# A two-layer post-LN network on one core: the same instructions, ordered by a planner with other costs and other shifts

## The chip, the core and the metric

The kernel runs on one core of one Trainium2 chip. The metric is device microseconds of one execution, here the median of 14 executions. Five engines of the core work side by side, each strictly in the order of its own queue: TensorE (PE in the profile; PEld is its loading of weights), VectorE (DVE), ScalarE (ACT), GpSimd (POOL) and SyncE (SP), which here only issues DMAs. Semaphores tie the queues together.

## The reference, cut to what matters

x has 8 batches of 512 tokens of 128 features, in float32. Four blocks follow each other, each with a residual sum and a LayerNorm behind it.

```python
x = L0_attn_x
x = _layernorm(x + _L0_attn_ref(x, ...))   # linear attention, then its own FFN
x = _layernorm(x + _L0_ffn_ref(x, ...))    # first mixture of experts
x = _layernorm(x + _L1_attn_ref(x, ...))   # softmax attention with rotary positions
x = _layernorm(x + _L1_ffn_ref(x, ...))    # last mixture of experts

# _L0_attn_ref: 16 heads of 64, 64 random features
qf = ratio * (exp(q_dash - diag - max_over_features) + EPS_KERN)
kf = ratio * (exp(k_dash - diag - max_over_all) + EPS_KERN)
kv = einsum('bnhm,bnhd->bhmd', kf, v)
num = einsum('bnhm,bhmd->bnhd', qf, kv)
den = einsum('bnhm,bhm->bnh', qf, sum(kf, axis=1))
out1 = _layernorm(x + attn_out)
h = elu(out1 @ W1 + b1)                    # 512 wide
return _layernorm(out1 + h @ W2 + b2)

# _L0_ffn_ref: 8 experts of width 64, the best 2 of each token
gates = _top_k_softmax(cos_scores + route_scores, 2)
h = gelu(einsum('bsd,edh->bseh', x, w1) + b1)
out = einsum('bse,bsed->bsd', gates, einsum('bseh,ehd->bsed', h, w2) + b2)

# _L1_attn_ref: 16 heads of 8
q, k = q * cos + rotate_half(q) * sin, k * cos + rotate_half(k) * sin
attn = softmax(einsum('bhqd,bhkd->bhqk', q, k) / sqrt(8))
out = einsum('bhqk,bhkd->bhqd', attn, v)   # then @ wo.T + bo

# _L1_ffn_ref: 8 experts of width 176, the best 2 of each token, and a shared expert
h = silu((x @ w1 + b1) * (x @ w3 + b3))    # per expert
y = sum over the 2 chosen experts of weight * (h @ w2 + b2)
return y + silu((x @ sw1 + sb1) * (x @ sw3 + sb3)) @ sw2 + sb2
```

## The kernel before, in words

**Stages.** 512 tokens of a batch are four blocks (NT) of 128 tokens by 128 features.

- *Keys.* `keys` runs once for all eight batches at the start: keys, their features and their sums, in scratch memory that is later used again (matmuls at L677, L687 and L716, VectorE at L684 and L693).
- *First layer, per batch* (`linear_attention_and_ffn`, stage 0): for each of the four blocks query features (PE L921, L931; ACT square and exponential; VectorE reductions L928 and L937; POOL product L945; VectorE L951), transposes (L961) and eight matmuls with the folded keys (L969); then a LayerNorm (`moments` and `layernorm`: VectorE L874 and L883, POOL power L876), an FFN (PE L994, L1005) and two more LayerNorms.
- *First mixture, per batch* (`first_mixture`, stage 1): transposes (L629, in the helper `transpose4`, which every stage uses), a router (L1040 and a row of short VectorE steps), one Gelu over all hidden units, gates spread over rows by DMA, matmuls L1075, L1089, L1091.
- *Attention, per batch* (`softmax_attention`, stage 2): projections (PE L1115; the rotary steps on VectorE and POOL L1121, L1122; VectorE and POOL L1127 split each value into a high part and a rest), four DMAs that write the parts to DRAM (`put`, L1104), eight that read them back as a layout of 32 rows per head (`get`, L1107), and the value projection (L1137). Then sixteen steps of four score matmuls on 32 rows each (L1183), two exponentials on ACT (L1189) and eight value matmuls (L1195); after each four steps transposes and a normalisation (L1202 to L1208); at the end the output projection (L1155) with its residual sum (L1161).
- *Last mixture.* Batches 0 to 3 and 4 and 5 are two groups in which tokens are sorted by expert (`sort`, stage 3: router L1309, counting matmuls L1563, eight indirect DMAs of POOL that scatter 128 token rows each to DRAM, L1506, and the shared expert, L1594 and L1603). When a group is sorted, `tiles` (stage 4) runs over tiles of 256 sorted rows: SP fetches the tile's expert weights (L1528) and rows, PE transposes (L1657) and multiplies (L1663, L1671), `gated` is between (VectorE L1548, L1552), and SP stores the rows. `combine` (stage 5) gathers each token's two rows with eight indirect DMAs of POOL (L1514) and adds them (L1690). Batches 6 and 7 go through `dense_mixture` (stage 3) instead: all experts for all tokens (PE L1364, L1389, VectorE L1375).

**The planner.** No instruction is issued where it is written. `Schedule` records each call, or each group of calls inside `nc.together()`, as a `Work` with its engine, a planned duration `us`, for DMAs a time `lands` until the data have landed, and the works before it, found from overlapping operands. `nc.do` records a DMA with a duration and landing time written by hand. A work also has a `part`: the stage and the batch or group. Stage 6 is the layout of the last mixture's weights, stage 7 the folded keys of a batch, and None is the rest.

`issue` takes the works in the order that `order` returns. This has three steps. `latest_alone` walks back from the due time of each work (40 us per batch) and gives its latest start, were it alone. To this `order` adds a shift per part from the table `URGENT`. `forward` then plans: each engine has a list of ready works, sorted by this urgency; again and again the earliest possible start is taken, among equals the most urgent, and the PSUM banks (8 banks, handed to works as they start) are assigned on the way.

```python
best = self.forward([u + shift[w.part] for u, w in zip(urgency, self.works)])
...
start, found, own = max(free[e], at[i]), (), ()
...
free[e] = start + us
done = start + max(us, w.lands)
```

`ROUNDS` is 0, so there is no search when the kernel is built: table and costs fix the order. The costs are in `Schedule.us` by engine and operation, `HANDOVER` (from one engine to another), `KEPT` (within one) and `REFILL` (PE changing between a full tiling and a 32-wide one). A planned start is not a time on the chip: it only sets the order in each queue, and the chip waits by semaphores wherever the plan was wrong.

Line numbers in this document up to the result are those of this kernel.

Of the kernel before, what the change touches and what calls it, by code (L numbers as in the profile page):

```python
# [84 lines left out]
URGENT = {  # L85
    (0, 0): 4.8, (0, 1): 6.8, (0, 2): -10.9, (0, 3): 9.3, (0, 4): 10.3, (0, 5): 17.3, (0, 6): 1172, (0, 7): 48.3,
    (1, 0): -1314.2, (1, 1): -963.6, (1, 2): 66.8, (1, 3): -32.6, (1, 4): -720.6, (1, 5): 37.5, (1, 6): 70.3,
    (1, 7): 692.6, (2, 0): -832.2, (2, 1): -87.5, (2, 2): -790.6, (2, 3): -167.1, (2, 4): -29.3, (2, 5): 50.4,
    (2, 6): -1456.9, (2, 7): -6.2, (3, 0): 52.7, (3, 1): 77.9, (3, 2): 703.5, (3, 3): 72.2, (3, 4): -20.5,
    (3, 5): 856.5, (3, 6): 600.2, (3, 7): 580.1, (4, 0): -19, (4, 1): 11.1, (5, 0): 131.5, (5, 1): 134.1,  # L90
    (5, 2): -1202, (5, 3): 1752.2, (5, 4): 2071, (5, 5): 1790.6, (6, 0): -359.3, (7, 0): -253.4, (7, 1): -263,
    (7, 2): 384.7, (7, 3): 186.4, (7, 4): -1273.5, (7, 5): -8.4, (7, 6): 784, (7, 7): 744.1, None: 19.1,
}
# [8 lines left out]
class Work:  # L102


    def __init__(self, engine):
        self.engine, self.calls, self.us, self.lands = engine, [], 0.0, 0.0
        self.before, self.after = set(), []
        self.tiles, self.part = set(), None
        self.outs, self.apart = 1, None


class Schedule:
# [4 lines left out]
    KEPT = {"PE": 0.0, "DVE": 0.12, "ACT": 0.13, "POOL": 0.12, "SP": 0.0}  # L117
    REFILL = 0.1
    NAMES = {"tensor": "PE", "vector": "DVE", "scalar": "ACT", "gpsimd": "POOL", "sync": "SP"}

# [67 lines left out]
    @staticmethod  # L188
    def us(engine, method, args, kwargs, work):

        aps = [a for a in (*args, *kwargs.values()) if isinstance(a, bass.AP)]
        n = max(math.prod(a.shape[1:]) for a in aps)
        if method == "dma_start":
            us = max(0.1, math.prod(aps[0].shape) * 4 / 300e3)
            work.lands = 2.3 + us
            return us if engine == "SP" else 0.4
        if engine == "PE":
            n = math.prod(args[0].shape[1:])
            if method == "transpose":
                return 0.11  # L200
            return 2 * max(0.1115, n / 1200 + 2.5e-3)
        if engine == "DVE":
            pointed = any(isinstance(a, bass.AP) and a.shape[-1] == 1 for a in args[2:])
            return 0.07 + n * 1.03e-3 + (0.06 if pointed else 0.0)
        if engine == "ACT":
            if any(a is AF.Gelu or a == AF.Gelu for a in args[2:]):
                return 4.5
            each = (kwargs.get(k) for k in ("bias", "scale"))
            return 0.07 + n * 0.83e-3 + 0.1 * sum(isinstance(a, bass.AP) for a in each)
        if method == "tensor_tensor" and args[3] == ALU.pow:  # L210
            return 1.0
        if method == "memset":
            return 0.1 + n * 0.75e-3
        return 0.1 + n * 2.26e-3
# [121 lines left out]
    def forward(self, urgency):  # L336
# [7 lines left out]
        clear = [0.0] * BANKS  # L344
        tiling, span, starts = None, 0.0, []
        free = dict.fromkeys(self.HANDOVER, 0.0)
        open_, at, ready = [len(w.before) for w in works], [0.0] * len(works), {e: [] for e in free}
# [3 lines left out]
        for _ in works:  # L351
            best = None
            for e, waiting in ready.items():
                kept, found_here = set(), None
                for entry in waiting:
# [4 lines left out]
                    for n in works[i].tiles:  # L360
# [13 lines left out]
                        if place is None:  # L374
                            start = NEVER
# [18 lines left out]
            if e == "PE":  # L394
                if self.tilings[i][0] != tiling or start > free[e]:
                    us += self.REFILL
                tiling = self.tilings[i][1]
            free[e] = start + us
            done = start + max(us, w.lands)
# [56 lines left out]
def kernel(ctx: ExitStack, tc: tile.TileContext, i: dict, out: bass.AP):  # L456
# [652 lines left out]
    def projections(xb, b=None):  # L1109
# [3 lines left out]
        for n, name in ((0, "q"), (1, "k")):  # L1113
# [10 lines left out]
            if b is not None:  # L1124
# [3 lines left out]
                for a, half in enumerate((high, r)):  # L1128
                    rows_d = halves_d[b, n].rearrange("p (u v) n -> p u v n", v=2)
                    nc.do(  # L1130
                        "sync", put, (rows_d[:, :, a] if n == 0 else rows_d[:, a],), (half,),
                        1.7, 4.0, ("halves", b, n),
                    )
# [30 lines left out]
    def softmax_attention(b, dst):  # L1164
# [3 lines left out]
        for j in range(4):  # L1168
            for n, to in ((1, kx), (0, qx)):
                nc.do(  # L1170
                    "sync", get, (to[:, j, :].bitcast(F32),),
                    (halves_d[b, n].rearrange("(r j) c n -> r j c n", j=4)[:, j],), 0.85, 3.2,
                )
# [3 lines left out]
        def probabilities(j, kt):  # L1177

            halves = [nc.banks(2, 4 * (kt % 2) + 2 * a) for a in range(2)]
            with nc.together(0.3):  # L1180
                for g in range(4):
# [429 lines left out]
    def tiles(n, end, group, rows_d, weights_of):  # L1611
# [37 lines left out]
        for j in range(most):  # L1649
            which, first = (listed[0:1, k, j : j + 1] for k in range(2))  # L1650
            w, x = weights_of.next(), tile2("m_x").rearrange("p (t d) -> p t d", d=D)
            nc.do("sync", fetch_weights, (w,), (w_d, which), 0.9, 4.5)
            nc.do("sync", fetch_tokens(group), (x,), (rows_d, first), 0.9, 3.3, ("tiles", group))
            xt = psb("xt")[:, 0:TR]
# [23 lines left out]
            )  # L1678
            nc.do("sync", store_tokens(group), (rows_d,), (y, first), 0.9, 3.3, ("tiles", group))

# [167 lines left out]
```

## Time and profile before

| what | value |
|---|---|
| median of 14 runs | 1201.43 us (1194.74 to 1209.97) |
| the profiled execution | 1207.79 us; span from first to last instruction 1205.9 us |
| mean granted TensorE clock | 0.942 of full speed |
| HBM read, written | 80.81 MB, 55.41 MB; 113 GB/s over the span |
| exponentials of the scores (ACT L1189) | 256 of 1030 ns: 245.5 us |
| value matmuls (PE L1195) | 1024 of 664 ns, overlapping: 157.7 us |
| score matmuls (PE L1183) | 512 of 537 ns, overlapping: 77.9 us |
| product with the key sums (POOL L945) | 32 of 2428 ns: 77.7 us |
| scatters and gathers (POOL L1506, L1514) | 48 of 1012 ns and 48 of 1043 ns |
| chain that ended last | PE 19% of the span, DVE 9%, issue 3%, ACT 2%, others 1% or less |

The profile is of one execution; its own time lies 6.4 us above the median. A busy share is the time in which at least one instruction of an engine was under way. PE's matmuls overlap in the pipeline, so the mean of one is longer than what a row of them costs each. The chain of work that ended last leaps over long stretches here, because nearly every step of it was released by an instruction that was itself ready early; so the reading goes by stretches and by what each PE instruction waited for.

The stretches in order: up to about 210 us the keys; from there to about 930 us the first layer of one batch, the attention of another and, late, sorted tiles overlap; the sorted tiles run from 767 to 1120 us; from 930 to 1010 us the last sort and the start of attention of batch 6; to 1150 us attention of batches 6 and 7 beside tiles and the dense mixture of batch 6 (L1364 from 1057 us); and then the last dense mixture.

### The profile page before, as it was taken

The page shows a single profiled execution, that of the slowest core. Times are in us where ns is not written, and L with a number is a line of the kernel's source. Part 1 is how long each engine was busy: PE and PEld are TensorE (multiplying, and loading weights), DVE is VectorE, ACT ScalarE, POOL GpSimd, SP SyncE. Part 2 cuts the span into 40 slices and gives each one's busy share as a digit, 9 for nine tenths or more (in the row PEclk, how much of TensorE's full clock was granted, in tenths as well). Part 3 has the DMA queues.
Part 4 walks back from the last instruction along what each step waited for, and adds up shares of the span by engine and source line. Part 5 has one row for each costly group of instructions (what it writes and reads, how often), then busy time and mean ns, then how long its engine had stood idle before and what let it go on. Part 6 is the DMA issues. An engine that isn't in the chain of part 4 may idle for free. (4 is left out here: it accounts for less than half of the span.)

```text
span 1205.9 us, 16926 instructions
## 1 busy us (share of the span) xinstructions
PE 1077.6 (89%) x5764; PEld 610.1 (51%) x5764; DVE 869.6 (72%) x1935; ACT 717.5 (60%) x959; POOL 443.5 (37%) x381
## 2 busy tenths in 40 slices
PE   8999999898889998999997997999898757899994
PEld 4444444674654554554454454466652523555553
DVE  5866666879997599497689579469765682674795
ACT  2354355465448758767765664876467646667652
POOL 0234222243444262253373533214344671210362
PEclk9999999999889999998998898899988967999998
DMA  7029901123051041033133105455713351574241
GB/s 219 27 52 307 323 12 71 62 84 81 27 184 44 19 169 51 27 130 101 34 123 114 44 35 180 147 146 163 237 36 104 96 195 51 155 235 132 68 117 57
DMA packets 104605, 134.40 MB, mean 111 GB/s; under 512 B 19474, under 2 KB 62285, under 8 KB 104513
## 3 DMA queue, kind: packets, MB, share of 16 engines
q1 hardware_dynamic: 101137, 126.41, 33.3%
q0 software_dynamic: 3072, 6.30, 1.8%
q8 instruction: 47, 0.77, 0.3%
q10 hardware_dynamic: 304, 0.56, 0.2%
q14 instruction: 45, 0.37, 0.1%
HBM read 80.81 MB, written 55.41 MB: 113 GB/s over the span
## 5 line engine op out<-in xcount | busy, mean ns | idle before, releaser
L1189 ACT ACTIVATE scratch<-ps 128x1024 f32<-128x1024 f32 x256 | 245.5, 1030 | 64.9 <-PE ps L1183 45.5
L1195 PE MATMUL ps<-scratch,vv 128*32 128x512 f32 x1024 | 157.7, 664 | 6.5 <-ACT scratch L1189 3.9
L945 POOL TENSOR_TENSOR scratch<-scratch 128x1024 f32<-128x1024 f32 x32 | 77.7, 2428 | 154.3 <-ACT scratch L942 126.7
L1183 PE MATMUL ps<-qx,kx 32*128 32x512 f32 x512 | 77.9, 537 | 29.6 <-ACT scratch L1189 15.0
L682 ACT ACTIVATE scratch<-ps 128x1024 f32<-128x1024 f32 x32 | 32.7, 1023 | 91.8 <-PE ps L677 91.8
L1183 PEld LDWEIGHTS ps<-qx,kx 32*128 32x128 f32 x512 | 29.8, 196 | 112.5 <-ACT scratch L1189 51.1
L969 PEld LDWEIGHTS ps<-scratch 128*128 128x128 f32 x512 | 62.9, 198 | 19.3 <-issue 12.7
L969 PE MATMUL ps<-scratch 128*128 128x128 f32 x512 | 66.7, 285 | 6.0 <-DVE f_ln_ve L874 3.9
L921 PE MATMUL ps<-wq,scratch 128*128 128x512 f32 x128 | 65.9, 627 | 2.8 <-ACT scratch L926 1.1
L931 PE MATMUL ps<-wqf,scratch 128*128 128x512 f32 x128 | 65.2, 620 | 0.3 <-DVE scratch L941 0.3
L1663 PE MATMUL ps<-scratch 128*128 128x256 f32 x228 | 60.6, 406 | 3.7 <-DVE scratch L1548 3.0
L693 DVE SCALAR_TENSOR_TENSOR scratch<-k_ssq,ps 128x1024 f32<-128x1024 f32 x32 | 38.8, 1213 | 33.3 <-PE ps L687 26.0
L1506 POOL DMA_INDIRECT x_d<-scratch,slots x48 | 48.6, 1012 | 37.0 <-DVE f_nb L939 12.8
L677 PE MATMUL ps<-scratch 128*128 128x512 f32 x128 | 60.2, 613 | 1.2 <-ACT scratch L669 0.7
L876 POOL TENSOR_TENSOR f_ln_rs<-f_ln_ve,nhalf 128x4 f32<-128x4 f32 x24 | 28.2, 1175 | 86.4 <-DVE f_ln_ve L874 72.7
L1514 POOL DMA_INDIRECT scratch<-x_d,slots x48 | 50.1, 1043 | 25.2 <-issue 13.3
L716 PE MATMUL ps<-scratch,x_sb 128*128 128x512 f32 x128 | 59.2, 595 | 0.0
L687 PE MATMUL ps<-scratch 128*128 128x512 f32 x128 | 58.6, 600 | 0.0
L937 DVE TENSOR_REDUCE f_mxq<-ps 128x16 f32<-128x1024 f32 x32 | 38.9, 1215 | 21.3 <-PE ps L931 10.0
L725 POOL TENSOR_TENSOR scratch<-scratch 128x1024 f32<-128x1024 f32 x7 | 16.5, 2364 | 100.2 <-PE ps L687 76.2
L684 DVE TENSOR_REDUCE k_ssq<-scratch 128x16 f32<-128x1024 f32 x32 | 38.9, 1215 | 19.8 <-ACT scratch L682 19.8
L1663 PEld LDWEIGHTS ps<-scratch 128*128 128x128 f32 x228 | 43.3, 203 | 15.6 <-DVE scratch L1548 4.2
(290 smaller groups left out, 2529.8 us busy)
## 6 DMA issues: line engine op xcount, KB each, us to landing
halves_d<-scratch SPq DMA_DIRECT2D x32, 512.0 KB
scratch<-w_d SPq DMA_DIRECT2D x38, 386.0 KB
x_d<-scratch SPq DMA_DIRECT2D x28, 512.0 KB
scratch<-g_d SPq DMA_DIRECT2D x68, 128.0 KB
qx<-halves_d SPq DMA_DIRECT2D x32, 256.0 KB
kx<-halves_d SPq DMA_DIRECT2D x32, 256.0 KB
scratch<-x_d SPq DMA_DIRECT2D x38, 128.0 KB
x_d<-scratch SPq DMA_DIRECT2D x38, 128.0 KB
```

What stands on the lines that cost most here:

```text
L677: nc.tensor.matmul(kp_ps[:, a, :], xT[:, t * P : (t + 1) * P], wk[:, a * 512 : (a + 1) * 512], start=True, stop=True,)
L687: nc.tensor.matmul(dp_ps[:, a, :], xT[:, t * P : (t + 1) * P], wkf[:, a * 512 : (a + 1) * 512], start=True, stop=True,)
L716: nc.tensor.matmul(xp_ps[:, a, :], x_of(b)[:, t, :], ek[:, t, a * 512 : (a + 1) * 512], start=(t == 0), stop=(t == NT - 1),)
L921: nc.tensor.matmul(qp[:, a, :], xT[:, t * P : (t + 1) * P], wq[:, a * 512 : (a + 1) * 512], start=True, stop=True,)
L931: nc.tensor.matmul(dp[:, a, :], xT[:, t * P : (t + 1) * P], wqf[:, a * 512 : (a + 1) * 512], start=True, stop=True,)
L945: nc.gpsimd.tensor_tensor(pr, eq, zr[:, 0:HM], ALU.mult)
L969: nc.tensor.matmul(at_ps[:, 0:D], qnT[:, c, :], kvo[:, c, :], start=(c == 0), stop=(c == 7))
L1183: nc.tensor.matmul(halves[g // 2][:, g % 2, :], kx[quarter, j, kt * P : (kt + 1) * P], qx[quarter, j, :], start=True, stop=True, tile_posi ...
L1189: nc.scalar.activation(pr[:, 2 * a : 2 * a + 2], sc, AF.Exp, scale=1.0 / math.sqrt(HD2))
L1195: nc.tensor.matmul(av[32 * g : 32 * g + 32, :], vv[:, kt, head_columns(4 * g + j)], pr[:, g, :], start=(kt == 0), stop=(kt == NT - 1), til ...
L1514: inst = tc.nc.gpsimd.indirect_dma_start(out=to, out_offset=None, in_=rows_d, in_offset=bass.IndirectOffsetOnAxis(ap=slots_, axis=0))
L1663: nc.tensor.matmul(to, w[:, c : c + P], xf, start=True, stop=True)
```

## The change

All calls, operands and dependences stay. What changes is what the planner is told:

- the table `URGENT`: 64 other shifts;
- a new term: VectorE's planned work becomes longer by 0.7 of the time in which it overlaps the last planned POOL `tensor_tensor` (`SHARED`, `shares`, `shared`);
- the planned cost of every DMA by `dma_start`: 0.45 us of its queue, landing after 2.4 us and 1 us for each 100,000 elements, in place of at least 0.1 us and 2.3 us and 1 us for each 300 KB;
- VectorE's reciprocals 0.06 us longer;
- the costs by hand of `put` (1.7 and 4.0 us to 0.6 and 4.2), `get` (0.85 and 3.2 to 0.6 and 4.4), the fetch of weights (0.9 and 4.5 to 0.4 and 4.2), the fetch and the store of rows (0.9 to 0.4), and the four score matmuls (0.3 to 0.335).

```diff
 URGENT = {
-    (0, 0): 4.8, (0, 1): 6.8, (0, 2): -10.9, (0, 3): 9.3, (0, 4): 10.3, (0, 5): 17.3, (0, 6): 1172, (0, 7): 48.3,
-    (1, 0): -1314.2, (1, 1): -963.6, (1, 2): 66.8, (1, 3): -32.6, (1, 4): -720.6, (1, 5): 37.5, (1, 6): 70.3,
...
-    (7, 2): 384.7, (7, 3): 186.4, (7, 4): -1273.5, (7, 5): -8.4, (7, 6): 784, (7, 7): 744.1, None: 19.1,
+    (0, 0): -50.3, (0, 1): -68.4, (0, 2): -44.4, (0, 3): 45.9, (0, 4): 9.7, (0, 5): 244.3, (0, 6): 1789,
+    (0, 7): 819.9, (1, 0): -1119.5, (1, 1): -1339.6, (1, 2): 82.9, (1, 3): -73.4, (1, 4): -541.6, (1, 5): 348.9,
...
+    (7, 1): 436.8, (7, 2): 707.9, (7, 3): 442.5, (7, 4): -1380.9, (7, 5): -634.9, (7, 6): 1112.9, (7, 7): 550.9,
+    None: -76.1,
 }
@@ class Schedule
     REFILL = 0.1
+    SHARED = 0.7
@@ us
         if method == "dma_start":
-            us = max(0.1, math.prod(aps[0].shape) * 4 / 300e3)
-            work.lands = 2.3 + us
-            return us if engine == "SP" else 0.4
+            work.lands = 2.4 + math.prod(aps[0].shape) / 100e3
+            return 0.45
...
-            return 0.07 + n * 1.03e-3 + (0.06 if pointed else 0.0)
+            return 0.07 + n * 1.03e-3 + (0.06 if pointed or method == "reciprocal" else 0.0)
...
+        work.shares = method == "tensor_tensor"
@@ forward
+        shared = (0.0, 0.0)
...
+            elif e == "DVE":
+                us += self.SHARED * max(0.0, min(start + us, shared[1]) - max(start, shared[0]))
+            elif w.shares:
+                shared = (start, start + us)
@@ projections, softmax_attention
                     nc.do(
                         "sync", put, (rows_d[:, :, a] if n == 0 else rows_d[:, a],), (half,),
-                        1.7, 4.0, ("halves", b, n),
+                        0.6, 4.2, ("halves", b, n),
...
-                    (halves_d[b, n].rearrange("(r j) c n -> r j c n", j=4)[:, j],), 0.85, 3.2,
+                    (halves_d[b, n].rearrange("(r j) c n -> r j c n", j=4)[:, j],), 0.6, 4.4,
...
-            with nc.together(0.3):
+            with nc.together(0.335):
@@ tiles
-            nc.do("sync", fetch_weights, (w,), (w_d, which), 0.9, 4.5)
-            nc.do("sync", fetch_tokens(group), (x,), (rows_d, first), 0.9, 3.3, ("tiles", group))
+            nc.do("sync", fetch_weights, (w,), (w_d, which), 0.4, 4.2)
+            nc.do("sync", fetch_tokens(group), (x,), (rows_d, first), 0.4, 3.3, ("tiles", group))
...
-            nc.do("sync", store_tokens(group), (rows_d,), (y, first), 0.9, 3.3, ("tiles", group))
+            nc.do("sync", store_tokens(group), (rows_d,), (y, first), 0.4, 3.3, ("tiles", group))
```

## The prediction

> **What bounds the kernel now.** I read four views in turn: the page's busy shares, the busy time by stretch, the timeline of single stretches, and the sources of single lines.
>
> ```profile
> span 1205.9 us, 16926 instructions
> PE 1077.6 (89%) x5764; PEld 610.1 (51%) x5764; DVE 869.6 (72%) x1935; ACT 717.5 (60%) x959; POOL 443.5 (37%) x381
> ...
> PEclk9999999999889999998998898899988967999998
> ```
>
> TensorE (PE) is busy 89% of the span, but a busy PE is not a PE at its peak, so I count its work. Back to back at full clock the chain of waits shows eight 128x128 matmuls in 0.89 us, six of 128x256 in 1.30 and four of 128x512 in 1.72. All groups priced like this (0.90 for eight of L1195, 0.30 for four of L1183) are an estimated 936 us. Starts of neighbouring groups lie 48 us further apart in small steps under 0.25 us (changes between full and 32-wide tilings above all), 98 us are true waits at full clock, and stretches at half clock cost 109 us more; about 15 us are the two ends. The clock records have 20 stretches at 0.50, 141 us together, which is the mean of 0.942 again: (1 - 0.942) / 0.5 x 1206 = 140. In them PE did 66.6 us of full-clock work, so 66.6 of the 109 us is the clock and 42 is waiting. Waits are thus 98 + 42 = 140 us, and the clock adds 66.6 / 140 = 0.47 us for each.
>
> ```profile
> 0.00:210.00 210.00, 202.11 (x615) 91.83 (x616) 137.88 (x186) 91.78 (x94) 55.26 (x34) 1.00 0.47 145
> ...
> 750.00:930.00 180.00, 161.34 (x1016) 102.42 (x1018) 118.04 (x309) 123.07 (x179) 63.29 (x69) 0.93 0.46 139
> 930.00:1010.00 80.00, 53.37 (x274) 28.14 (x272) 52.47 (x167) 42.25 (x65) 49.20 (x51) 0.74 0.40 129
> 1010.00:1150.00 140.00, 133.56 (x841) 79.87 (x838) 90.74 (x221) 98.98 (x148) 26.50 (x22) 0.99 0.45 134
> 1150.00:1206.00 56.00, 37.92 (x179) 23.50 (x178) 39.34 (x93) 22.60 (x43) 24.99 (x21) 0.92 0.28 86
> ```
>
> Columns: stretch, its length, busy us (and instructions) of PE, weight loads, VectorE (DVE), ACT and POOL, clock, DMA. The keys stage (first row) is full: no order can save much there. The worst stretch is 930 to 1010: PE busy 53 of 80 us, clock 0.74. No engine is full there; it is a passage of short dependent steps, in which attention of batch 6 waits for its projections and the last sort for its router.
>
> ```profile
> 872.84 1.07 PE L1195 MATMUL ps<-scratch,vv 128*32 128x512 f32 x8
> ...
> 876.61 2.93 PE L1663 MATMUL ps<-scratch 128*128 128x256 f32 x6 [2.70 <-DVE scratch L1548]
> ...
> 879.33 1.06 PE L961 MATMUL ps<-ident,scratch 128*128 128x128 f32 x4
> ```
>
> What an order can lose is seen here: PE waits 2.7 us for an L1663 while the L961 behind it had its inputs. Engines take their queues strictly in order, so a late head holds back all behind it.
>
> **The change part by part.** The instructions are the same: 4869 pieces of work with the same dependences, 17 activation tables loaded before and after. Only the order on the five engines and the PSUM banks differ, because the planner's costs and 64 shifts differ. I laid every instruction of the trace on its piece of work, and then both orders beside each other.
>
> *1. Late heads that go.* For each gap over 0.3 us before a PE group I looked whether one of the eight groups behind had all inputs. Such gaps hold 94.7 us that a ready group could have taken. For 39.4 us of it the new order has that ready group first (the L961 above is one). Term: -39.4 us of waits.
>
> *2. Waits that come.* For each PE group that needs another engine's result of an earlier PE group, I took the steps between at their durations in the trace, without queues, less the PE work that lies between the two. What is left is a wait that the order cannot avoid: 85.4 us before, 86.9 us after. 21.5 us go and 23.0 come. They come where the mixture of batch 7 starts behind L1005 of its first layer (L1005 to L629 and L1040: +8.9), at the last routers (L1309 to L1563: +4.3), at L931 to L961 (+2.3) and L994 to L1005 (+2.6); they go at L1115 to L1183 (-5.1), the sorted tiles (-3.3) and L1594 to L1603 (-4.2). The 23.0 is a floor. Measured waits are 140 against 85.4, a factor of 1.64, so the other end is 38. I take the middle, 30: nothing puts the truth nearer to one end.
>
> *3. Clock.* Net waits -39.4 + 30.5 = -9, and 0.47 of it by the clock: -4. Both ends: (-39.4 + 23) x 1.47 = -24 and (-39.4 + 38) x 1.47 = -2.
>
> *4. Changes of tiling.* They go from 363 to 377. A change cost about 0.10 us (L1195 to L1183 0.095 in the mean, L1183 to L1195 0.136): +1.4; the ends, +1.3 to +1.9, don't matter.
>
> *5. Batch 6.* Its projections (L1115) stand at 758.9 us of PE work instead of 763.8, ahead of L1005 and the router of batch 5. VectorE must have done 815 us of its work before the first scores now and 819 before, so the start gains little beyond term 2. I take 0; ends -7 (L1115 earlier by 4.9, x 1.47) and the first rival.
>
> *6. Queues of SP and POOL.* SP's 491 issues are moved with their steps; L1104 takes 548 ns and L1107 594 ns in the median, and the queue is far from full. The scatters of batches 0 and 1 come about 45 to 60 us of PE work earlier, behind which POOL has slack. Cost 0: what they feed (the tiles) starts at the same place, 628 against 621 us of PE work. Ends -3 and +3, the mean length of three such issues of about 1.0 us.
>
> *7. The port term.* The plan now lengthens VectorE's work under a POOL tensor_tensor. It moves nothing by itself; its effect is in terms 1 and 2. Its accuracy can be read here.
>
> ```profile
> L883 DVE SCALAR_TENSOR_TENSOR f_ln_nm<-f_ln_mv,f_ln_rs x16: 147/155/2268, 247.5 to 970.9; 128x4 f32<-128x4 f32 x16
> ...
> L928 DVE TENSOR_REDUCE f_ssq<-scratch x32: 1149/1206/1220, 185.0 to 750.7; 128x16 f32<-128x1024 f32 x32
> ```
>
> Minimum, median, maximum in ns: L883 has two SBUF inputs and is held for up to 2.27 us; L928 has one and is never lengthened, though 16 of its 32 ran beside such a POOL instruction. Over the trace, VectorE lost 87 us to collisions. The new term, applied at the same places, would charge 157 us, much of it to reductions that lose nothing, and too little to short instructions that lose most (L883 1.4 charged of 8.9).
>
> The Trainium skill, page "SBUF — State Buffer", section "Who interferes with whom", says that the shared ports are an exclusive lock for a whole instruction, taken by a VectorE instruction with two SBUF inputs, and not by one with a single input outside the two-port modes. Both rows agree with it, and it speaks against this change: a share of the overlap is the wrong shape. Whoever trusts the rule alone would give the new order no better judgement than the old, terms 1 to 3 as nothing, and 1203; by the measured late heads it is 1190.
>
> **The sum.** -9 - 4 + 1.4 + 0 = -11.6 us. The profiled execution took 1207.8 us (span 1205.9), 6.4 above the median of 1201.4 of the 14 runs, so it becomes 1196.2 in its own terms, and 1190 against the median. One wait of the profile may belong to that difference:
>
> ```profile
> 1001.29 3.91 ACT L1189 ACTIVATE scratch<-ps 128x1024 f32<-128x1024 f32 x4 [9.24 <-remote]
> ```
>
> Its inputs had landed 8 us earlier, and nothing in the trace released it. Two like it stand at 746 to 750 and 869 to 877; all three fall on POOL's scatters (L1506).
>
> **Rivals.**
>
> *A. The passage of batch 6 grows (slower).* At 769 us of PE work, L1603 now needs 815 us of VectorE's work instead of 809 and 374 us of POOL's instead of 365, since L1121, L1122 and L1127 of batch 6 and gathers stand ahead. For it: POOL was busy 49 of 80 us here and VectorE's chains run through it. Against it: the first scores need 4 us less. If both come in series, 6 + 9 = 15 us of waiting, 22 with the clock: 1190 + 22 = 1212. It decides from 8 us on, where 8 x 1.47 eats the gain.
>
> *B. As many late heads as before (no change).* With 38 us of new waits the sum is -1.4 x 1.47 + 1.4: -1, or 1200. For it: the equal sums of unavoidable waits, 85.4 and 86.9. Against it: costs for SP and DMA were far off before (1.7 us planned for L1104, 0.55 measured) and are close now.
>
> *C. The stalls at the scatters don't return (faster still).* They are 4.7, about 7 and 8.5 us. Without them, and with term 3 at its good end: 1201 - 24 - 20 + 1 = 1158; with half of that, 1173. Against it: nothing shows that the median run has them.
>
> *D. The end of attention 7 is late.* L1155 stands 10.5 us of PE work before L629 of the last mixture, 17.4 before. The steps between took 7.5 us (1130.5 to 1138.0), so about 2 us of reserve remain of 9. Each further us is paid in full: with 5 us of VectorE backlog, 1190 + 3 = 1193 and still faster.
>
> **How the numbers follow.** No change means within 0.3%, about what a measurement of this kernel can tell: 1197.8 to 1205.0. My forecast, with D: 0.42. C: 0.16. B: 0.12. A and other growth: 0.30. So faster 0.58, same 0.12, slower 0.30. The forecast's own range is 1177 to 1198 (its ends -24 and -2). The range for 8 in 10 reaches into C and A: 1165 to 1214.
>
> **What would show it.** Right: PE waits down by some 9 us, time at half clock from 141 to about 132, mean clock 0.945 or more; the L961 ahead of the L1663 near 860; the stretch between the projections of batch 6 and its steady scores no longer than 50 us. Term 2 is wrong if L629 and L1040 of batch 7 wait over 6 us each. A shows as POOL or VectorE named before L1603 and L1183 there, for over 8 us more than now. B shows as equal waits at other lines. The port term does work if VectorE's L883, L874 and L1552 lose clearly less than their 8.9, 8.4 and 5.8 us. I am wrong altogether if PE's waits change by over 25 us.

## The result and the profile after

The changed kernel takes 1239.93 us in the median (1235.88 to 1245.78, 10 runs) against 1200.5 us before (47 runs). The ratio is 1.0338, 95% interval 1.0314 to 1.0362: 39 us slower, where the prediction had it 11 us faster and its widest range ended at 1214 us. Its profiled execution took 1240.87 us (span 1239.0), 33.1 us of span more than the one before. In the changed kernel every line behind the head of `Schedule` has moved by 7 (L503 is now L510, L1183 is L1190). The table `URGENT` holds 50 shifts, not the 64 of the text ahead.

The page of the changed kernel, its parts 1 and 2:

```profile
span 1239.0 us, 16930 instructions
PE 1083.8 (87%) x5764; PEld 611.9 (49%) x5764; DVE 859.1 (69%) x1935; ACT 718.5 (58%) x959; POOL 442.0 (36%) x381
...
PEclk9999899998898999898999988899997967989997
```

No engine has more to do. VectorE even has 10 us less, and TensorE's 6 us more go with a lower clock (0.936 in the mean against 0.942). What has grown is idle time. The busy time by stretch (stretch, its length, PE, weight loads, VectorE, ACT, POOL, clock, DMA) says where:

```profile
0.00:210.00 210.00, 185.38 (x509) 83.61 (x510) 124.26 (x164) 78.45 (x80) 52.83 (x33) 0.98 0.46 135
...
750.00:930.00 180.00, 159.52 (x991) 108.92 (x989) 137.71 (x354) 112.46 (x174) 59.06 (x63) 0.95 0.50 155
930.00:1010.00 80.00, 53.82 (x302) 25.90 (x302) 47.78 (x153) 49.90 (x70) 50.41 (x48) 0.80 0.38 117
1010.00:1150.00 140.00, 125.42 (x750) 70.72 (x754) 79.35 (x217) 96.87 (x138) 29.18 (x33) 0.90 0.44 137
```

In the first 210 us TensorE did 509 instructions in place of 615. That is the keys stage, of which the prediction said that no order could save much. It did not ask what an order could lose there. The later stretches hold other work than before, since by then everything comes some 20 to 40 us later, so they do not tell more.

A sharper reading puts the two profiles beside each other by work done: when had TensorE got through its first 25, 100, 200 us of work (at the prices of the prediction), and how much later was that than before? This table holds the answer for the changed kernel and for the kernels of the experiments below. It is worked out from the traces, in us:

| TensorE work done | changed | changed, again | changed, loads first | before, zeros first | before, new transfer cost | before, port term | changed, port term off |
|---|---|---|---|---|---|---|---|
| 25 | 5.4 | 5.5 | 5.6 | -1.1 | 6.5 | 0.6 | 6.6 |
| 100 | 7.5 | 7.6 | 7.7 | -1.1 | 6.5 | 2.7 | 6.6 |
| 125 | 18.6 | 18.5 | 9.1 | 12.1 | 19.7 | 4.1 | 19.5 |
| 200 | 21.7 | 21.7 | 12.3 | 12.1 | 19.6 | 7.3 | 18.9 |

So 21.7 of the 33 us are lost while the keys are made, in steps: 5.4 at the very start, 11 between 100 and 125 us of work, and some 5 in small ones. Behind the keys the difference rises to 37.6 us at 525 us of work, falls to 28.3 at 750 and ends at 33. What TensorE waited for longest in its first 215 us, before (engine and line, what released it, us in total, times, longest):

```profile
PE ps L629 <- DMA x_sb<-in_x_dram: 3.5, 1, 3.5
```

and after:

```profile
PE ps L636 <- DMA x_sb<-in_x_dram: 12.4, 3, 7.5
PE ps L684 <- ACT scratch L689: 4.7, 4, 1.2
PE ps L664 <- DVE k_mxt L699: 2.9, 1, 2.9
```

The largest item is a wait for x itself, three times in place of once. The longest of the three, in the order of time (start, us, and in brackets the idle time before and what ended it):

```profile
145.31 1.09 PE L636 MATMUL ps<-ident,x_sb 128*128 128x128 f32 x4 [7.48 <-DMA x_sb<-in_x_dram]
```

The queue of SP shows why. Before (start, us in the queue, line, transfer, how many):

```profile
85.86 0.38 SPq L503 DMA_DIRECT2D x_sb<-in_x_dram  x1
...
99.62 1.62 SPq L1420 DMA_DIRECT2D x_d<-scratch  x2
101.28 1.29 SPq L1408 DMA_DIRECT2D w_d<-scratch  x1
102.62 1.27 SPq L1420 DMA_DIRECT2D x_d<-scratch  x1
107.80 0.33 SPq L670 DMA_DIRECT2D xT_d<-scratch  x1
108.48 0.39 SPq L503 DMA_DIRECT2D x_sb<-in_x_dram  x1
```

and after:

```profile
91.90 0.38 SPq L510 DMA_DIRECT2D x_sb<-in_x_dram  x1
...
93.73 3.54 SPq L1427 DMA_DIRECT2D x_d<-scratch  x4
97.32 1.20 SPq L1415 DMA_DIRECT2D w_d<-scratch  x1
98.56 5.97 SPq L1427 DMA_DIRECT2D x_d<-scratch  x5
...
129.22 2.91 SPq L1427 DMA_DIRECT2D x_d<-scratch  x3
...
135.15 3.19 SPq L677 DMA_DIRECT2D xT_d<-scratch  x1
138.44 0.39 SPq L510 DMA_DIRECT2D x_sb<-in_x_dram  x1
```

L1427 (L1420 before) writes zeros into the buffers of the sorted rows, 28 transfers of 512 KB each. Before, eight to ten of them stood between two loads of x, and SP was idle from 104 to 108 us, ready for the next. After, all 28 stand in one row with only a few writes of L1415 among them, each takes about 1.2 us of the queue as soon as the first few are under way, and the next load of x, which TensorE needs at 138 us, is issued at 138.4. TensorE has it 7 us later.

### The profile page after: what moved, and what is told of

The parts are those of the page before. It is cut to its first block, busy times and chain, and to the rows that moved or that the text cites. A ratio compares the mean times of both kernels' runs of the same rounds, so it can differ in the third digit from the quotient of the medians.

```text
span 1239.0 us, 16930 instructions
## 1 busy us (share of the span) xinstructions
PE 1083.8 (87%) x5764; PEld 611.9 (49%) x5764; DVE 859.1 (69%) x1935; ACT 718.5 (58%) x959; POOL 442.0 (36%) x381
## 5 line engine op out<-in xcount | busy, mean ns | idle before, releaser
L1202 PE MATMUL ps<-scratch,vv 128*32 128x512 f32 x1024 | 154.0, 656 | 8.5 <-issue 3.0
L1190 PE MATMUL ps<-qx,kx 32*128 32x512 f32 x512 | 76.6, 526 | 24.2 <-ACT scratch L1196 11.5
L689 ACT ACTIVATE scratch<-ps 128x1024 f32<-128x1024 f32 x32 | 32.8, 1024 | 96.7 <-PE ps L684 96.7
L1190 PEld LDWEIGHTS ps<-qx,kx 32*128 32x128 f32 x512 | 29.0, 192 | 103.4 <-ACT scratch L1196 43.5
L976 PE MATMUL ps<-scratch 128*128 128x128 f32 x512 | 63.9, 278 | 1.8 <-DVE scratch L1017 0.8
L1521 POOL DMA_INDIRECT scratch<-x_d,slots x48 | 48.4, 1009 | 38.5 <-DVE scratch L1697 11.8
L700 DVE SCALAR_TENSOR_TENSOR scratch<-k_ssq,ps 128x1024 f32<-128x1024 f32 x32 | 38.9, 1216 | 33.1 <-PE ps L694 30.2
L636 PE MATMUL ps<-ident,scratch 128*128 128x128 f32 x224 | 39.5, 297 | 19.7 <-ACT scratch L892 6.7
L883 POOL TENSOR_TENSOR f_ln_rs<-f_ln_ve,nhalf 128x4 f32<-128x4 f32 x24 | 25.7, 1069 | 85.8 <-DVE f_ln_ve L881 85.0
```

The lines of the kernel that those rows point to most:

```text
L976: nc.tensor.matmul(at_ps[:, 0:D], qnT[:, c, :], kvo[:, c, :], start=(c == 0), stop=(c == 7))
L1190: nc.tensor.matmul(halves[g // 2][:, g % 2, :], kx[quarter, j, kt * P : (kt + 1) * P], qx[quarter, j, :], start=True, stop=True, tile_posi ...
L1202: nc.tensor.matmul(av[32 * g : 32 * g + 32, :], vv[:, kt, head_columns(4 * g + j)], pr[:, g, :], start=(kt == 0), stop=(kt == NT - 1), til ...
L1521: inst = tc.nc.gpsimd.indirect_dma_start(out=to, out_offset=None, in_=rows_d, in_offset=bass.IndirectOffsetOnAxis(ap=slots_, axis=0))
```

## The experiments

Ratios are against the kernel before on the same chip; they leave out the profiled executions, which the medians include. TensorE's work is counted at the same prices throughout.

### Is it the planner's cost of a transfer?

The line that a `dma_start` is charged by is the only part of the change that moves TensorE's order in the keys stage. With the old line in the changed kernel, TensorE's first 217 groups stand as before; with the new line in the kernel before, they stand as in the changed one. Both were run.

```diff
@@ changed kernel, us
-            work.lands = 2.4 + math.prod(aps[0].shape) / 100e3
-            return 0.45
+            us = max(0.1, math.prod(aps[0].shape) * 4 / 300e3)
+            work.lands = 2.3 + us
+            return us if engine == "SP" else 0.4
```

> The changed kernel with one line of the planner undone: a dma_start costs SP again its bytes at 300 GB/s (at least 0.1 us) in place of 0.45 us; table, port term and the costs by hand stay as changed. With this, TensorE's first 217 groups (the keys stage) stand as in the kernel before. Theory 1 (the keys stage lost 21.7 us of the 33 between the two profiled executions, because 28 writes of zeros now stand ahead of the loads of x on SP's queue): the keys stage is as before and the time about 1240 - 22 = 1218 us, give or take 10 since the rest is planned anew. Theory 2 (the loss lies in the new table and the port term, and what the keys stage loses is waited for later anyway): 1240 us.

Measured: 1241.23 us, ratio 1.0362 (1.0312 to 1.0411), no gain. In its trace the keys are 6.8 us behind the kernel before at 200 us of work in place of 21.7, so 15 us did come back there. But the planner ordered the rest anew, and that lost 30 us by the end. As a test of time it missed; as a test of where the keys' loss comes from it did not.

```diff
@@ kernel before, us
-            us = max(0.1, math.prod(aps[0].shape) * 4 / 300e3)
-            work.lands = 2.3 + us
-            return us if engine == "SP" else 0.4
+            work.lands = 2.4 + math.prod(aps[0].shape) / 100e3
+            return 0.45
```

> The kernel before with only that line of the planner changed: a dma_start costs SP 0.45 us and lands after 2.4 us and 1 us for each 100,000 elements. TensorE's first 217 groups then stand as in the changed kernel. Theory 1: about 1200 + 22 = 1222 us, with two waits of TensorE for x in the keys stage. Theory 2: 1200 us, within the 10 us that a new plan of the rest may make.

Measured: ratio 1.0301 (1.0246 to 1.0356), 1234 us, 12 us over theory 1: the new plan of the rest lost too. The trace shows the two steps of the table: 6.5 us at the start, 13.2 between 100 and 125. So this one line makes both.

### Is it the order in SP's queue, or TensorE's?

The next two kernels keep the orders of TensorE, VectorE, ACT and POOL, and the banks, exactly. The planner's list is replaced by a fixed one, in which 43 transfers of SP in the keys stage have changed places (the texts below count 48).

```diff
@@ order
-        self.makespan, self.starts, self.bank = best
-        return [i for _, i in self.starts]
+        self.bank = dict(enumerate(PLACED))
+        return LINE
```

> The changed kernel with its order on TensorE, VectorE, ScalarE and GpSimd; on SP's queue alone the 48 transfers around the writes of zeros stand in the order of the kernel before (two or three writes between the others, so the loads of x are no longer behind 28 writes). Theory 1: the waits for x at 137.6 us go, and with them 11.1 to 14 us: 1226 to 1229 us. Theory 3 (inside the keys stage it is the order of TensorE and VectorE that costs, and the loads only look late): the same 1240 us, at most 3 us less.

Measured: 1227.28 us, ratio 1.0277 (1.0201 to 1.0353). The median is theory 1's, but its four times spread from 1222 to 1237 us and the interval reaches from theory 1 (about 1.023) to theory 3 (1.031 to 1.033), so the time does not decide. The trace does. The waits of TensorE up to 215 us:

```profile
PE ps L636 <- DMA x_sb<-in_x_dram: 5.1, 2, 3.4
PE ps L684 <- ACT scratch L689: 4.7, 4, 1.2
PE ps L664 <- DVE k_mxt L699: 2.9, 1, 2.9
```

The wait of 7.5 us is gone, the others stand as they were. Of all 1233 groups of TensorE only this one moved by more than 4 us against its neighbour in the changed kernel, and at 200 us of work the keys are 12.3 us late in place of 21.7.

> The other way round: the kernel before, with those 48 transfers of SP in the order of the changed kernel and all other queues untouched. Theory 1: TensorE waits for x near 130 us and the time is 1200 + 11 to 14 = 1211 to 1214 us. Theory 3: 1200 us.

Measured: 1216.71 us, ratio 1.0163 (1.0114 to 1.0211), a little more than theory 1 said and clear of theory 3. In the kernel before, with nothing but SP's queue changed:

```profile
PE ps L629 <- DMA x_sb<-in_x_dram: 13.9, 2, 10.7
```

Theory 1 holds both ways: in the traces the row of writes ahead of the loads costs 9 to 13 us, and TensorE's order has no part in it.

### Do keys and rest add up?

A fixed list again: one kernel's order for what it issues in its first 200 us of TensorE work, the other's order for everything behind.

```diff
@@ order
-        self.makespan, self.starts, self.bank = best
-        return [i for _, i in self.starts]
+        self.bank = dict(enumerate(PLACED))
+        return LINE  # of one kernel up to 200 us of TensorE work, then of the other
```

> All works that the kernel before issues in its first 200 us of TensorE work (the keys stage, on all five queues) stand in its order and banks; everything behind stands in the order of the changed kernel. If the 21.7 us of the keys stage are lost for good: 1240 - 22 = 1218 us. The SP queue alone gave 1227, so 9 us more would be the other parts of the keys order (5.4 us at its start, 2.9 us later). Rival: what stands behind the keys loses the same however the keys go, because it follows from another part of the order; then still 1227.

Measured: 1186.32 us where the kernel before took 1180.32, ratio 1.0060 (1.0034 to 1.0087), less than the 1.015 that 1218 us would have been. This chip was 20 us faster for the kernel before too, so nothing could be added up yet, and the changed kernel was run again, with the mirror image and the kernel before, on one chip.

> The kernel before, unchanged, for a trace on the same chip as the runs beside it. The four last profiles came from a chip on which the kernel before took 1180 us, and they show none of the waits of ScalarE that nothing in the trace releases (14.4 us in the first profile of before, all while GpSimd scattered or gathered). If those waits are what sets chips apart: a time near 1200 with such waits, or near 1180 without them. If they don't matter: the time is not tied to them.

> The changed kernel, unchanged, beside the others on one chip. On a chip with the unexplained waits a ratio of 1.034 to before as measured; on a chip without them theory 1 (21.7 us of keys and some 7 to 11 of the rest, none of it from those waits) gives 1180 + 21.7 + 9 = 1211 us or a ratio of 1.026; if the unexplained waits make the difference between the kernels, a ratio under 1.02.

> The works that the changed kernel issues in its first 200 us of TensorE work stand in its order, everything behind in the order of the kernel before: the mirror image of the kernel that gave 1.006. If the 21.7 us of the keys stage are lost for good: a ratio of 1.018. If the keys stage matters only together with the rest of the changed order: under 1.010.

> The order of the kernel before for the keys stage, of the changed kernel behind it, now beside the changed kernel on one chip. If keys and rest simply add: the ratio of the changed kernel less 0.018. On the chip without unexplained waits 1.006 as measured; on one with them 1.012 to 1.020, since the profile of the changed kernel has 18.7 us of such waits of ScalarE against 14.4 before.

Measured on that chip (kernel before 1203.84 us):

| kernel | median us | ratio | interval |
|---|---|---|---|
| before, again | 1203.06 | 0.9994 | 0.9967 to 1.0021 |
| changed, again | 1245.09 | 1.0337 | 1.0301 to 1.0374 |
| keys of changed, rest of before | 1230.39 | 1.0222 | 1.0184 to 1.0261 |
| keys of before, rest of changed | 1221.32 | 1.0133 | 1.0096 to 1.0171 |

They add: 0.0222 + 0.0133 = 0.0355 against 0.0337. The keys are two thirds of the loss (a little more than the 1.018 that was expected of them), the rest of the order is one third, some 16 us here. The keys' part comes out at 21.8 us in the trace of the third kernel, 21.7 in both traces of the changed one, and none of it is made up later.

### Is it what the change is about, or that the old order was left?

The rest of the order was still open: 7 to 16 us that no single wait explains. Theory 4 is that the old table of shifts fits the old costs, so that any step away costs. Five kernels let the planner plan anew. The first two ran on the chip where the kernel before takes 1180 us; the changed kernel was not run there, so their ratios are not strictly comparable with its 1.034.

```diff
@@ kernel before: the new port term alone
+    SHARED = 0.7
...
+        work.shares = method == "tensor_tensor"
...
+            elif e == "DVE":
+                us += self.SHARED * max(0.0, min(start + us, shared[1]) - max(start, shared[0]))
+            elif w.shares:
+                shared = (start, start + us)
```

> The kernel before with the new port term alone (VectorE's planned work longer by 0.7 of its overlap with a tensor_tensor of GpSimd); costs of transfers and table as before. Theory 4 (the old table fits the old costs; any new plan brings as many late heads as an order picked without looking, some 30 us more than before has): 1210 to 1235 us. Theory 5 (the term judges collisions better or does nothing): 1195 to 1203 us. The rule on shared ports, that only some instructions are held, speaks for no gain in either case.

Measured: ratio 1.0487 (1.0442 to 1.0532), the worst of the parts: 58 us where theory 4 had 10 to 35 (its 1210 to 1235 us were meant for a chip of 1200, a ratio of 1.008 to 1.029). The keys lose 7.3 us; TensorE there, in its first 215 us:

```profile
PE ps L683 <- ACT scratch L688: 4.7, 4, 1.2
```

(L677 and L682 of the kernel before.) This wait is in every kernel planned with the term and in none planned without. VectorE's L693, with an input from PSUM and one from SBUF, is charged for running beside POOL's L725. The trace of before, where 11 of its 32 ran beside one, shows that it loses nothing:

```profile
L693 DVE SCALAR_TENSOR_TENSOR scratch<-k_ssq,ps x32: 1199/1211/1222, 18.9 to 182.7; 128x1024 f32<-128x1024 f32 x32
```

Minimum, median and maximum lie within 23 ns. In the keys this plan keeps the orders of TensorE and ACT; what differs is VectorE's order and the PSUM banks that groups are given. The inputs of the waiting group had been there for 7 us; its bank was still being read:

```profile
93.78 1.02 ACT L688 ACTIVATE scratch<-ps 128x1024 f32<-128x1024 f32 x1 [1.50 <-PE ps L683]
94.86 1.98 PE L683 MATMUL ps<-scratch 128*128 128x512 f32 x4 [1.17 <-ACT scratch L688]
```

So a charge for collisions, some of which do not happen, brought other banks and with them a wait. That the charge on L693 is what turns the plan was not tried by itself.

```diff
@@ kernel before: the new table alone
-    (0, 0): 4.8, (0, 1): 6.8, (0, 2): -10.9, (0, 3): 9.3, (0, 4): 10.3, (0, 5): 17.3, (0, 6): 1172, (0, 7): 48.3,
...
+    (0, 0): -50.3, (0, 1): -68.4, (0, 2): -44.4, (0, 3): 45.9, (0, 4): 9.7, (0, 5): 244.3, (0, 6): 1789,
...
```

> The kernel before with the 64 new shifts alone; all costs as before, so the keys stage keeps its order on TensorE for its first 217 groups. Theory 4: 1210 to 1235 us, all of it behind the keys. Rival: the new shifts are the better ones, and only the transfers' new cost spoilt them: 1190 to 1200 us.

Measured: ratio 1.0323 (1.0281 to 1.0366), all of it behind the keys, as theory 4 said, and a little over its range taken as a ratio.

```diff
@@ kernel before, order: each shift with a random number (1 is the seed; the second kernel has 4)
-        shift, chance = {p: URGENT.get(p, 0.0) for p in parts}, random.Random(1)
+        noise = random.Random(1); shift, chance = {p: URGENT.get(p, 0.0) + noise.gauss(0.0, 3.0) for p in parts}, random.Random(1)
```

> The kernel before with a random number (normal, width 3 us) added to each of its 64 shifts; all costs as before. Its keys stage keeps TensorE's first 223 groups. Theory 4 (the old table fits the old costs, and leaving it costs whatever the reason): the planner of before rates this order 1105 us against 1080 for its own; orders it rated 1099 to 1127 measured 1.001 to 1.032, so a ratio of about 1.012. By the costs of the changed kernel it is rated 1167 against 1144 for before and 1121 for after, so a planner that is right there would give it about 1.02 or more and after less than 1. Rival (the loss of after comes from what the change is about, not from leaving a fitted order): 1.00.

> The same with other random numbers; the old costs rate it 1125 us. Theory 4: a ratio of 1.015 to 1.035. Rival: 1.00, since nothing of the change is in it.

Measured: 1.0202 (1.0149 to 1.0255) and 1.0307 (1.0259 to 1.0354). Random numbers of 3 us on shifts of up to 2071 us cost nearly as much as the change. The rival, that only the change's own parts cost, falls: leaving the order was enough, twice. The first lies above the 1.012 that its rating by the old costs stood for, and where a planner right by the new costs would have had it; the second is in the range of theory 4. By the old costs the random numbers of seeds 0 to 15 give orders of 1094 to 1134 us, so these two are not picked from one end, and none reaches the 1080 of before.

```diff
@@ changed kernel
-    SHARED = 0.7
+    SHARED = 0.0
```

> The changed kernel with the port term off (0 in place of 0.7), new table and new transfers' costs kept. The 1.34 us waits of TensorE for ScalarE's L689 in the keys stage, which came in every plan with the term and in none without, should go (some 5 to 7 us of the keys), the waits for x stay. But the new table was fitted together with the term: the old costs rate this order 1183 us, worse than any run so far, so theory 4 gives 1.04 to 1.06 in all. Rival (the term is what spoils the order): 1.015 to 1.025.

Measured: ratio 1.0613 (1.0564 to 1.0661), the slowest of all, just over the range of theory 4. The waits for ACT's L689 in the keys are gone, as expected, and the row of zeros is still there (14.9 us of waits for x), so the keys get back 2.8 us and not 5 to 7. The rest loses far more. That fits a table found together with the term (with it the planner rates the changed order 1121 us by the new costs, and no order below better), but how the table was found is not on record. The term alone costs, and taking it from the changed kernel costs too.

The planner's own rating of an order puts this together. Here each measured order was rated by the planner with the old costs and with the new ones; these figures are the planner's, and only the ratio in the last column is measured. Lines with two chips give the one nearer to 1200 us.

```
order                               old costs  new costs  measured ratio
before                                 1080       1144       1
before to 525, changed to 750, before  1099       1144       1.0065
before, zeros first                    1101       1144       1.0163
before with noise 1                    1105       1167       1.0202
keys of changed, rest of before        1116       1138       1.0222
before, new table                      1125       1184       1.0323
before with noise 4                    1125       1184       1.0307
keys of before, rest of changed        1127       1130       1.0133
before, new transfer cost              1135       1163       1.0301
changed, old transfer cost             1141       1133       1.0362
changed, loads first                   1142       1121       1.0277
before, port term                      1155       1171       1.0487
changed                                1161       1121       1.0337
changed, port term off                 1183       1200       1.0613
```

The old costs rank these orders nearly as the chip does (rank correlation 0.84); the new costs hardly do (0.33), and they put the changed order 2% ahead of the old one where the chip puts it 3.4% behind. They can't see the row of zeros at all: the third line is rated like the first. And of the 64 us that they add to the old order, 59 come from the port term alone. Without that term the new costs rank these orders as well as the old ones do (0.86), and put the changed order at 1112 us against 1085 for the old one, on the right side. So the term is what makes the planner take the slower order for the faster.

### A faster kernel from both?

Between 525 and 750 us of work the profile of the changed kernel made up 9 us, so this stretch of its order was put into the kernel before, as a fixed list.

> The order of the kernel before up to 525 us of TensorE work, of the changed kernel from there to 750, and of the kernel before again from there. Between these two points the changed kernel's profile made up 9.3 us (37.6 us behind at 525, 28.3 at 750). If that is a property of the order: 1200 - 9 = 1191 us. If the stretch only gained because it started late and other queues had run ahead: 1200. If the second seam costs (buffers and banks change owners): up to 1210.

> The order of the kernel before to 525 us of TensorE work, of the changed kernel to 750, of before again behind it, on another chip perhaps. On the chip without the unexplained waits of ScalarE it was 1.001. If this stretch of the changed order is better on a chip that has those waits: 0.993 or less; if not: 1.000 to 1.005.

Measured: 1.0011 (0.9982 to 1.0040) on one chip, 1.0065 (1.0039 to 1.0090) on another. The stretch is no better in the old order. The second pair of profiles of both kernels, taken on one chip, shows no gain to begin with: there the changed kernel is some 37 us behind at 525 us of work and some 40 at 750. So the 9 us belong to the first pair of executions. No kernel here beats the kernel before.

## Why the prediction was wrong

**The start of the reading.** "No order can save much there" of the keys stage was true and was taken for "nothing can change there". No term of the sum asks what a full stage can lose. It lost 21.7 us: 5.4 with the new transfer cost at its start, some 11 by the row of writes (step 6), some 5 in waits that come with the port term (step 7).

**6, queues of SP and POOL (0, ends -3 and +3).** This is the step that failed most, by 9 to 13 us. It looked at how long one issue takes and found the queue "far from full", and at where the scatters stand. It did not look at what had moved ahead of the loads of x: 28 transfers of 512 KB in one row. The median issue of other lines (548 and 594 ns) is no price for these, which take about 1.2 us each once several are under way. Rival B counted the new costs for SP as an improvement ("far off before and are close now"): right for L1104, wrong for the zeros, for which the old line, 512 KB at 300 GB/s or 1.75 us, had been the better one.

**1 and 2, late heads that go, waits that come (-39.4 and +30).** The 39.4 us were counted one way only. The same count on the trace of the changed kernel finds 123.6 us of waits that a ready group among the next eight could have taken, against 94.7 before. So if 39.4 went, 68.3 came; and the whole growth of TensorE's gaps over 0.3 us, 205.2 to 232.6, is late heads by that count. What is left of the gaps stayed equal, 110.5 and 109.0, as term 2 had said of its floor (85.4 and 86.9). But these sums cover the keys too: some 20 us of the growth lie there, where groups behind a late load of x are ready, so they are the loss named above, seen once more. Behind the keys the late heads are some 11 us longer in this pair of profiles and some 27 in the second pair, and about half of that where the ready group must also find its PSUM banks free. The error was to take the new waits from the unavoidable ones, scaled by 1.64, when the new order was bound to have late heads of its own, in places that the old trace can't show. The two kernels with noise have 121.6 and 103.5 us of them, and the old order's 94.7 (88.3 in its second profile) are the fewest of all 14 profiles taken on chips of its kind. That is what a selected order looks like; that it was selected is argued, not shown. The sign set for term 2 did not come: behind the keys no wait of L636 (L629 before) was over 4.0 us.

**3, the clock.** Right in its ratio and wrong in its sign: waits rose by 19.1 us (98.5 + 42.0 to 108.0 + 51.6) and the clock cost 8.8 more (66.6 to 75.4), 0.46 us for each against 0.47. Time at half clock went from 141 to 160 us.

**4, changes of tiling.** The small steps are 48.4 us before and after; nothing to see of the +1.4.

**5 and rival A, batch 6.** The wait at L1603 grew, as A said, but by less than its point of decision. TensorE's waits over the whole span, before:

```profile
PE ps L1603 <- DVE scratch L1552: 11.3, 2, 11.1
```

and after:

```profile
PE ps L1610 <- DVE scratch L1559: 14.6, 2, 13.9
```

From 725 to 825 us of TensorE work the changed kernel lost 5.5 us, in its second trace 5.0. A was right on the side and is a small part of the sum.

**7, the port term.** It does not "move nothing by itself": alone it costs 4.9%. What was said of its accuracy holds. VectorE's losses to collisions, counted as in the prediction, fell from 87 to 75 us (L883 from 8.9 to 5.3, L874 from 8.4 up to 10.5, L1552 from 5.8 up to 6.8), and TensorE's late heads grew meanwhile; that the one paid for the other is not shown. The rule that the prediction cites from the Trainium skill, page "SBUF — State Buffer", section "Who interferes with whom" (a VectorE instruction with one SBUF input, outside the two-port modes, does not take the lock), agrees with L693 above: 11 of its 32 ran beside L725, and all 32 durations lie within 23 ns.

**Rivals C and D, and B.** C fell: the waits of ACT that nothing releases are 18.7 us in the changed kernel's trace against 14.4. D fell: L1155 of batch 7 waits 0.0 us (its reserve was 10.5 - 7.5 = 3 us, not 2). B had "as many late heads as before", which was the right question with too kind an answer.

**What stays open.** Of the 11 to 16 us behind the keys, the late heads are shown as a sum. Which of the 50 shifts brings which was not taken apart, and with noise alone doing the same it may have no better answer. The 5.4 us at the start come with the new transfer cost; two waits lie there, L664 for a PSUM bank that VectorE's L699 still read (2.9 us) and a second group of transposes of x that now stands early (2 us more of L636), but neither was undone by itself.

## What to carry to other kernels

When a change replaces one order of the same work by another, count both ways: what the old trace shows as late will go, and as much or more can come where the old trace can't show it, and here two random neighbours of the order cost 2 to 3%, which is a first estimate for another new plan of this kernel. Before a queue is called far from full, list what has moved ahead of the transfers that the bound engine waits for, with its bytes; and check a new cost model by whether it ranks orders that have been measured, not by whether single costs come nearer to the trace.

## What the hardware showed that was not expected

One chip differed from the others in what happens while POOL scatters and gathers. On it the kernel before took 1180 us, and none of the four profiles taken there (all of other orders) has a wait of ACT that nothing in the trace releases. On the others it took 1200 to 1205 us, and all 14 profiles have such waits, 3.7 to 23.9 us of ACT in each, every one over 0.8 us beside an indirect DMA of POOL. That these waits make up the 20 us between the chips is not shown. One and the same order, keys of before and rest of changed, took 1186.32 us on the first and 1221.32 on another. There, the waits of ACT by what released them, and one of them in the order of time:

```profile
ACT scratch L1196 <- remote: 23.9, 8, 4.7
```

```profile
1001.41 0.97 POOL L1513 DMA_INDIRECT x_d<-scratch,slots  x1 [0.22 <-issue]
1002.69 0.99 POOL L1521 DMA_INDIRECT scratch<-x_d,slots  x1 [0.31 <-issue]
1005.38 0.75 DVE L1083 TENSOR_SCALAR scratch<-ps,cols 128x512 f32<-128x512 f32 x1 [6.95 <-remote]
1005.48 1.94 ACT L1196 ACTIVATE scratch<-ps 128x1024 f32<-128x1024 f32 x2 [4.73 <-remote]
```

VectorE and ACT stand still together here and go on within 0.1 us of each other. With the same order on chips of the slower kind, the long ones come back in the same places (9.2 us up to 1001 us in the profile of before, 9.3 in its second profile and in that of the kernel with zeros first), so they belong to the order as well as to the chip. What holds the engines there is open.

The second is the price of a transfer in a full queue: in the kernel before the first write of 512 KB took 0.45 us of SP's queue; in the changed one the writes in a row took about 1.2 us each, and a load of 256 KB issued behind them reached TensorE 7 us later.
